# Cross-attention kernel: prompts turned by VectorE, second context chunk turned before the first gram, first x loaded before the keys' weights

## The chip, the core and the metric

The kernel runs on one core of a Trainium2 chip. A core has five engines that run side by side and wait for one another through semaphores: TensorE (PE; its weight loads are shown apart as PEld), VectorE (DVE), ScalarE (ACT), GpSimd (POOL) and SyncE (SP), which here only issues DMAs. The metric is the time of one execution in microseconds (us), lower is better. Everything is float32.

## The reference

Eight batches; each has 112 queries of 320 channels (20 heads of 16) and a context of 375 tokens of 512 channels. The last four tokens of a context are "prompts", the 371 before them are text.

```python
q   = heads(x @ W_q);  k_t = heads(text @ W_k);  v_t = heads(text @ W_v)
probs_t  = softmax(q k_t^T * Dh**-0.5)
text_out = probs_t @ v_t
k_ip = heads(ip @ W_k_ip);  v_ip = heads(ip @ W_v_ip)
qsem = l2norm(probs_t @ text);  ip_n = l2norm(ip)
fused    = q k_ip^T * Dh**-0.5 + 0.5 * (qsem @ ip_n^T)
probs_ip = softmax(fused) * spatial_mask
out = (text_out + probs_ip @ v_ip) @ W_out + b_out + x
```

## The kernel before

**What is computed how.** The norm of `probs_t @ text` is not computed from that product. For each batch the kernel makes a gram matrix of the context tokens (`ctxT` times itself, tile `ug`), in which the four prompt tokens are replaced by their normalised and halved versions. Multiplying the exponentials of the scores with this matrix (the `ps_qd` matmuls, L776) then gives at once what the norms, the prompts' similarities, the softmax sum and the values need.

**Tiles and stages.** Contractions run over partitions, so the context, x and the prompts have to be turned (transposed) first: `ctxT` (512 channels as 128 partitions x 4, by 375 tokens), `xT`, and for the prompts `ipT` (raw, for their keys and values) and `ipnT` (normalised, for the gram). The 32 prompts of all eight batches (`ip_sb`, 32 x 512) are turned once, at the start. The context of batch 0 comes in three chunks of 128 tokens, the last one short (`ct`), each turned by four TensorE transposes into a PSUM bank `ps_c` (L435) and copied out, chunks 0 and 2 by ScalarE (L445), chunk 1 by VectorE (L443). The contexts of the later batches are turned by VectorE in 32 x 32 blocks.

The first gram has one bank for each row of chunks (L474): chunk column 0 needs chunk 0, column 1 chunks 0 and 1, column 2 all three and the prompts' columns, which GpSimd copies from `ipnT` (L468).

**What sets the order.** The order on TensorE, SyncE and VectorE is written out by hand: the prologue is a list of `next(...)` on generators, each of which yields after a piece of work, and an engine runs its instructions strictly in the order in which they were recorded. In the part that the change touches, TensorE does: `awake(4, 168)` (four matmuls on a constant, 168 columns wide, whose result nobody reads; they stand there ahead of the first data), the transposes of chunk 0, those of the raw prompts, the first block of the gram, the transposes of chunks 1 and 2, those of the normalised prompts, the other five blocks of the gram, then the first third of batch 0's queries (L371, from `xT` and `wq_sb`), keys (L568, `wk_sb`), more queries, scores (L705), values (L602, `wv_sb`). A float32 matmul is two entries in the trace, so four matmuls are listed as x8; a transpose is one entry.

All loads of the start but one stand in one SyncE queue: the context of batch 0, `wq_sb`, `wk_sb`, four loads of x into `xr_sb`, `wv_in`, the context of batch 1 (L160, L165). Only `ip_sb` goes through ScalarE's queue.

The kernel's bound in the steady part is TensorE: five groups of heads in each of eight batches, each with scores, `ps_qd` matmuls and, spread in between, the next batch's gram, keys and values. The change touches nothing there.

Of the kernel before, what the change touches and what calls it, by code (L numbers as in the profile page):

```python
# [20 lines left out]
def kernel(  # L21
# [14 lines left out]
    nc = tc.nc  # L36
    P = 128
# [7 lines left out]
    NE = E // P  # L45
# [5 lines left out]
    RG = 32  # L51
# [5 lines left out]
    N = B * NIP  # L57
# [5 lines left out]
    QN = P // RG  # L63
# [21 lines left out]
    def bank(name, spare=False):  # L85

        if spare:
            return ps_sc.tile([P, 512], F32, tag="sc", name=name)
        return ps_mm.tile([P, 512], F32, tag="mm", name=name)
# [22 lines left out]
    ip_sb = const.tile([N, E], F32, tag="ip_sb", name="ip_sb")  # L112
# [5 lines left out]
    def load_pairs(eng, t, w):  # L118

        w = w.rearrange("(p c) f -> p c f", c=5)  # L120
        eng.dma_start(t[0::2, :, :C], w[:, :3, :])
        eng.dma_start(t[1::2, :2, :C], w[:, 3:, :])

    def load_x_blocks(b, j):

        for a in range(QN):
            nc.sync.dma_start(
                xr_sb[a * RG : a * RG + S // QN, j, :, :XB],
                x[b, :, a * XB : (a + 1) * XB].rearrange("(q i) f -> i q f", q=QN),
            )  # L130
# [5 lines left out]
    def load_embed(eng, t, w):  # L136
        eng.dma_start(t[:, :, :C], w.rearrange("(p e) f -> p e f", e=NE))
# [9 lines left out]
    def chunk(t, e):  # L147
        return t.rearrange("t (p e) -> t e p", e=NE)[:, e, :]
# [38 lines left out]
    ident = const.tile([P, P], F32, tag="ident", name="ident")  # L187
# [2 lines left out]
    nc.gpsimd.memset(xr_sb, 0.0)  # L190

    load_pairs(nc.sync, wq_sb, w_q)
    load_embed(nc.sync, wk_sb, w_k)
    load_x_blocks(0, 1)
    load_embed(nc.sync, wv_in, w_v)
    load_ctx_blocks(1)

# [45 lines left out]
    ipT = const.tile([P, NE, N], F32, tag="ipT", name="ipT")  # L243
    ipnT = const.tile([P, NE, N], F32, tag="ipnT", name="ipnT")
# [19 lines left out]

    def normalised_prompts():

        def turned_prompts(src, n):
            ps = bank(f"ps_ipT{n}", spare=True)
            for e in range(NE):
                nc.tensor.transpose(  # L270
                    ps[:, e * N : (e + 1) * N], chunk(src, e), ident[:N, :N]
                )
            return ps[:, : NE * N].rearrange("p (e n) -> p e n", n=N)

        raw = turned_prompts(ip_sb, "r")
        yield

        sq = work.tile([N, E], F32, tag="ipn", name="ipsq", bufs=1)
        ss = small.tile([N, 1], F32, tag="ipss", name="ipss", bufs=1)
        nc.vector.tensor_tensor_reduce(  # L280
            out=sq, in0=ip_sb, in1=ip_sb, scale=1.0, scalar=0.0, op0=ALU.mult, op1=ALU.add,
            accum_out=ss,
        )
        nc.vector.tensor_scalar_max(ss, ss, EPS * EPS)
        rn = small.tile([N, 1], F32, tag="iprn", name="iprn", bufs=1)
        nc.scalar.activation(rn, ss, AF.Sqrt)
        nc.vector.reciprocal(rn, rn)

        ipn = work.tile([N, E], F32, tag="ipn", name="ipn", bufs=1)
        nc.vector.tensor_scalar(ipn, ip_sb, rn, 0.5, op0=ALU.mult, op1=ALU.mult)  # L290
        nc.vector.tensor_copy(ipT, raw)
        yield

        nc.vector.tensor_copy(ipnT, turned_prompts(ipn, "n"))
        yield

    def prompt_projections():
# [119 lines left out]
    def transposed_context(b):  # L417
        begin(b)
        s = st[b]
        ct, ctxT = s["ct"], s["ctxT"]  # L420
        if b > 0:

            for c in range(NT):
                some = slice(c * QN, (c + 1) * QN)
                nc.vector.transpose(  # L425
                    ctxT[:, :, c * P : (c + 1) * P].rearrange("p e (j i) -> p j e i", i=RG),
                    ct[:, some, :].rearrange("p j (k e) -> p j e k", e=NE),
                )
                yield
            return  # L430
        for c in range(NT):
            rows = min(P, TT - c * P)
            ps = bank(f"ps_c_{b}_{c}")
            for e in range(NE):
                nc.tensor.transpose(  # L435
                    ps[:, e * P : e * P + rows],
                    chunk(ct[:, c, :], e)[:rows],
                    ident[:rows, :rows],
                )
            o = ctxT[:, :, c * P : c * P + rows]  # L440
            i = ps.rearrange("p (e t) -> p e t", t=P)[:, :, :rows]
            if c == 1:
                nc.vector.tensor_copy(o, i)  # L443
            else:
                nc.scalar.copy(o, i)  # L445
            yield

    def awake(n, w):

        ps = bank(f"ps_w_{n}", spare=True)  # L450
        one = nc.const_aps.tensor(1.0, [P, w], F32)
        for _ in range(n):
            nc.tensor.matmul(ps[:, :w], one[:, :P], one, start=True, stop=True)
# [7 lines left out]
    def first_gram():  # L461

        ctxT = st[0]["ctxT"]
        banks = []
        for c in range(NT):
            banks.append(ps_qd.tile([P, 512], F32, tag="qd", name=f"ps_g_0_{c}"))
            if c == NT - 1:
                nc.gpsimd.tensor_copy(ctxT[:, :, TT:T], ipnT[:, :, :NIP])  # L468
                for xt in x_ring:
                    nc.gpsimd.memset(xt, 0.0)  # L470
            c0, c1 = c * P, min(c * P + P, T)
            for r in range(c + 1):
                for e in range(NE):
                    nc.tensor.matmul(  # L474
                        banks[r][:, c0 - r * P : c1 - r * P],
                        ctxT[:, e, r * P : (r + 1) * P],
                        ctxT[:, e, c0:c1],
                        start=(e == 0),
                        stop=(e == NE - 1),
                    )  # L480
                if c == NT - 1:
                    doubled(banks[r][:, : T - r * P], r, half[:, 0])
                yield
# [681 lines left out]

    across = [[(a, (a + k) % GROUP) for a in range(GROUP)] for k in range(1, GROUP)]
    prompts = normalised_prompts()
    context = transposed_context(0)
    products = first_gram()
    awake(4, 168)  # L1170
    next(context)
    next(prompts)
    next(prompts)
    next(products)
    next(context)
    next(context)
    next(prompts)
    run(("q", 0), lambda: project_queries(pairs[0]))
# [170 lines left out]
    for g in range(NG):  # L1349
# [6 lines left out]
        for j, _ in enumerate(multiplied(b, g)):  # L1356
# [17 lines left out]
            if g == 1 and j in (2, 3):  # L1374
                for a in ((3, 2), (1, 0))[j - 2]:
                    ps = ps_qd.tile([P, 512], F32, tag="qd", name=f"ps_s_{b}_{NG - 1}_{a}")
# [10 lines left out]
        n = (3, 3, 2, 1)[g]  # L1387
# [91 lines left out]
```

## Time and profile before

| | us |
|---|---|
| median of 3 runs | 414.4 (413.74 to 415.95) |
| the profiled execution's own time | 416.99 |
| its span, first to last instruction | 415.3 |
| first context chunk's transposes start on TensorE | 3.75 |
| first block of the gram starts | 5.53 |
| other blocks of the gram start | 9.77 |
| first queries start | 16.29 |
| VectorE turns x (`xT`) | 12.38 |

Times inside the execution are counted from the span's start. A row of the time line reads: start, time from the first to the end of the last, engine, line, operation, output and input, shape, count, and in brackets how long the engine stood idle before it and what ended that. Matmuls overlap in the pipeline, so one that is listed with 0.42 us may follow the one before it after 0.21 us; the distance of the starts is the pace.

### The profile page before, as it was taken

To read this page: it belongs to the slowest core of one execution; us is meant where nothing else is said; L and a number is where in the kernel's file an instruction comes from. 1 tells how busy PE (TensorE), PEld (TensorE's weight loads), DVE (VectorE), ACT (ScalarE), POOL (GpSimd) and SP (SyncE) were. 2 spreads that over 40 slices of the span, in tenths; PEclk is the share of its full clock that TensorE was granted. 3 is DMA by queue.
4 is the path that set the end of the run, shared out by engine and by line. 5 is a ranking of instruction groups with operands and counts; after the bars stand their busy time and mean duration, and the time that the engine had idled before them with its cause. 6 is when DMAs were issued, how large, how long until landed. Compare 5 with 4: busy or idle time off the path is not lost.

```text
span 415.3 us, 14115 instructions
## 1 busy us (share of the span) xinstructions
PE 409.0 (98%) x5484; PEld 320.7 (77%) x5484; DVE 339.1 (82%) x729; ACT 219.5 (53%) x733; POOL 130.0 (31%) x318
## 2 busy tenths in 40 slices
PE   8999999999999999999999999999999999999995
PEld 7866777788777877788677877788777987787883
DVE  4286788888899979898799988888798977889775
ACT  2364334746365453655448363653637563688773
POOL 4744203112071212612044120702117120545540
PEclk9999999999999999999999999999999999999999
DMA  7647655556654555455555555545544356544300
GB/s 215 149 123 166 203 145 149 138 145 167 173 152 135 153 141 137 115 137 163 138 131 134 138 152 140 149 107 165 140 127 113 95 166 160 131 121 135 104 2 29
DMA packets 46435, 56.95 MB, mean 137 GB/s; under 512 B 9405, under 2 KB 40961, under 8 KB 46368
## 3 DMA queue, kind: packets, MB, share of 16 engines
q1 hardware_dynamic: 46328, 55.99, 50.8%
q8 instruction: 43, 0.70, 0.8%
q14 instruction: 24, 0.20, 0.2%
q10 hardware_dynamic: 40, 0.07, 0.1%
HBM read 15.88 MB, written 1.39 MB: 42 GB/s over the span
## 4 chain that ended last, share of the span: by engine, by line
PE 93%; DVE 3%; DMA 1%; ACT 1%; issue 1%; DVEq 0%
PE ps_qd L776 39%; PE ps_v L602 15%; PE ps_s L705 11%; PE ps_k L568 10%; PE ps_g L518 7%; PE ps_q L371 4%; PE ps_o L993 3%; PE ps_g L474 2%; DVE junk L822 1%; DMA xg<-p 1%; DMA ct<-in_ctx_dram 1%; PE ps_c L435 1%; PE ps_k L584 1%; PE ps_k L559 0%; PE ps_a L981 0%
## 5 line engine op out<-in xcount | busy, mean ns | idle before, releaser
L776 PE MATMUL ps_qd<-u,xgT 32*112 32x168 f32 (+11 forms) x3840 | 216.1, 350 | 0.0
L776 PEld LDWEIGHTS ps_qd<-u,xgT 32*112 32x112 f32 x3840 | 183.8, 172 | 25.9 <-issue 0.5
L741 ACT ACTIVATE p<-ps_s,nmx 112x371 f32<-112x371 f32 x156 | 84.5, 579 | 82.9 <-DVE nmx L727 79.7
L757 DVE STREAM_TRANSPOSE xgT<-xg 128x512 f32<-128x512 f32 (+2 forms) x79 | 126.0, 1602 | 2.4 <-issue 1.8
L727 DVE TENSOR_REDUCE nmx<-ps_s 112x1 f32<-112x371 f32 x160 | 78.8, 537 | 24.7 <-PE ps_s L705 23.5
L822 DVE CUSTOM_DVE_ANT_0 junk<-ps_qd,p 112x371 f32<-112x371 f32 x146 | 79.3, 543 | 19.4 <-ACT pvs L789 3.6
L674 POOL COPY u<-vr 128x64 f32<-128x64 f32 x120 | 26.5, 239 | 140.6 <-PE ps_qd L776 104.1
L705 PE MATMUL ps_s<-kT,qm 32*112 32x375 f32 (+1 forms) x320 | 65.3, 495 | 0.0
L602 PE MATMUL ps_v<-wv_sb,ctxT 128*128 128x384 f32 (+1 forms) x192 | 63.1, 477 | 0.0
L602 PEld LDWEIGHTS ps_v<-wv_sb,ctxT 128*128 128x128 f32 x192 | 35.7, 190 | 21.9 <-DVE qm L381 0.5
L568 PE MATMUL ps_k<-ctxT,wk_sb 128*128 128x371 f32 x136 | 46.6, 487 | 0.0
L705 PEld LDWEIGHTS ps_s<-kT,qm 32*112 32x112 f32 x320 | 25.4, 171 | 12.8 <-issue 10.3
L568 PEld LDWEIGHTS ps_k<-ctxT,wk_sb 128*128 128x128 f32 x136 | 24.5, 189 | 13.5 <-ACT vext L609 0.2
L622 ACT COPY vr<-vext 32x240 f32<-32x240 f32 x88 | 34.2, 389 | 1.3
L609 ACT COPY vext<-ps_v 128x384 f32<-128x384 f32 (+1 forms) x24 | 11.2, 468 | 41.2 <-PE ps_v L602 41.2
L518 PE MATMUL ps_g<-ctxT 128*32 128x375 f32 (+11 forms) x672 | 30.4, 333 | 0.0
L518 PEld LDWEIGHTS ps_g<-ctxT 128*32 128x32 f32 x672 | 27.7, 110 | 2.0
L425 DVE STREAM_TRANSPOSE ctxT<-ct 128x512 f32<-128x512 f32 x21 | 23.1, 1112 | 3.4 <-DMA ct<-in_ctx_dram 3.4
L968 POOL TENSOR_TENSOR wv<-vip,w 112x1280 f32<-112x1280 f32 x6 | 14.8, 2468 | 26.6 <-DVE w L905 26.6
L743 ACT COPY ipl<-ps_s 112x4 f32<-112x4 f32 x140 | 23.1, 165 | 0.0
L490 ACT ACTIVATE ug<-ps_g 128x375 f32<-128x375 f32 (+2 forms) x24 | 8.3, 375 | 26.7 <-PE ps_g L518 10.4
L491 POOL TENSOR_TENSOR ug<-ug,half 128x128 f32<-128x128 f32 (+1 forms) x24 | 10.5, 449 | 29.7 <-ACT ug L490 29.7
(173 smaller groups left out, 348.6 us busy)
## 6 DMA issues: line engine op xcount, KB each, us to landing
xg<-p SPq DMA_DIRECT2D x156, 162.3 KB
u<-ug SPq DMA_DIRECT2D x122, 99.0 KB
ct<-in_ctx_dram SPq DMA_DIRECT2D x28, 176.0 KB
vip<-vipd SPq DMA_DIRECT2D x6, 560.0 KB
xr_sb<-in_x_dram SPq DMA_DIRECT2D x32, 35.0 KB
out_dram<-ob SPq DMA_DIRECT2D x8, 140.0 KB
x_sb<-in_x_dram SPq DMA_DIRECT2D x6, 140.0 KB
xg<-wv_sb SPq DMA_DIRECT2D x4, 162.3 KB
```

The source lines that it names most:

```text
L425: nc.vector.transpose(ctxT[:, :, c * P : (c + 1) * P].rearrange("p e (j i) -> p j e i", i=RG), ct[:, some, :].rearrange("p j (k e) -> p j ...
L518: nc.tensor.matmul(ps[c][q * RG : (q + 1) * RG, j * RG - c * P : T - c * P], ctxT[:, e, j * RG : (j + 1) * RG], ctxT[:, e, j * RG : T], st ...
L568: nc.tensor.matmul(ps[:, :TT], wk_sb[:, e, i * P : (i + 1) * P], s["ctxT"][:, e, :TT], start=(e == 0), stop=(e == NE - 1),)
L602: nc.tensor.matmul(ps[:, :w], ctxT[:, e, c * P : (c + 1) * P], wv_sb[:, e, :w], start=(e == 0), stop=(e == NE - 1),)
L622: copy(s["vr"][a * RG : (a + 1) * RG, q::QN].rearrange("p c g d -> p c (g d)"), s["vext"][q * RG : (q + 1) * RG, :, a * w : (a + 1) * w],)
L674: nc.gpsimd.tensor_copy(v, dealt(b, c, s["vr"][:, c * QN : (c + 1) * QN, g, :]))
L705: nc.tensor.matmul(ps[:S, :w], qm[a * RG : (a + 1) * RG, i, r, j * S : (j + 1) * S], s["kT"][a * RG : (a + 1) * RG, i, :w], start=True, st ...
L727: nc.vector.tensor_reduce(nmx, s["sc", g, a][:S, :TT], AX.X, ALU.max, negate=True)
L741: nc.scalar.activation(s["p", g][:, a, :], ps[:S, :TT], AF.Exp, bias=nmx)
L757: nc.vector.transpose(xT[:, j0:j1].rearrange("p j (k q) -> p q j k", q=QN), xg[:, :, j0 * RG : j1 * RG].rearrange("p q (j k) -> p q j k", ...
L776: nc.tensor.matmul(banks[a][:S, j * RG : UW], xT[a * RG : (a + 1) * RG, j, :S], region(b, c)[a * RG : (a + 1) * RG, q, j * RG - c * P :], ...
L822: nc.vector.tensor_tensor_reduce(out=junk, in0=ps[:S, :TT], in1=s["p", g][:, a, :], scale=1.0, scalar=0.0, op0=ALU.mult, op1=ALU.add, accu ...
```

## The change

Four edits, all ahead of the first scores:

- The prompts are turned by VectorE instead of TensorE. `turned_prompts` was four TensorE transposes into a PSUM bank and one VectorE copy out of it. It is now four VectorE block transposes of 32 x 128 each, which write straight into `ipT` or `ipnT`. As VectorE turns 32 x 32 blocks, 128 neighbouring channels of the prompts land in 32 partitions, one row group for each quarter of the channels. The placing of the channels is as before: channel 4 p + e in partition p, column e.
- Normalised prompts come first, raw ones after them, and the reciprocal and the scaling of the normalised prompts are recorded after the copy of context chunk 1.
- Context chunk 1 is turned ahead of the gram's first block.
- The four loads of x go ahead of `wk_sb` in SyncE's queue, and the four matmuls of `awake` are 200 columns wide instead of 168.

```diff
@@ -190,8 +190,8 @@
     load_pairs(nc.sync, wq_sb, w_q)
+    load_x_blocks(0, 1)
     load_embed(nc.sync, wk_sb, w_k)
-    load_x_blocks(0, 1)
     load_embed(nc.sync, wv_in, w_v)
@@ -264,16 +264,12 @@
-        def turned_prompts(src, n):
-            ps = bank(f"ps_ipT{n}", spare=True)
-            for e in range(NE):
-                nc.tensor.transpose(
-                    ps[:, e * N : (e + 1) * N], chunk(src, e), ident[:N, :N]
+        def turned_prompts(out, src):
+            for a in range(QN):
+                nc.vector.transpose(
+                    out[a * RG : (a + 1) * RG],
+                    src[:, a * P : (a + 1) * P].rearrange("n (p e) -> n e p", e=NE),
                 )
-            return ps[:, : NE * N].rearrange("p (e n) -> p e n", n=N)
-
-        raw = turned_prompts(ip_sb, "r")
-        yield
@@ -284,14 +280,15 @@
         nc.scalar.activation(rn, ss, AF.Sqrt)
+        yield
+
         nc.vector.reciprocal(rn, rn)
-
         ipn = work.tile([N, E], F32, tag="ipn", name="ipn", bufs=1)
         nc.vector.tensor_scalar(ipn, ip_sb, rn, 0.5, op0=ALU.mult, op1=ALU.mult)
-        nc.vector.tensor_copy(ipT, raw)
-        yield
-
-        nc.vector.tensor_copy(ipnT, turned_prompts(ipn, "n"))
+        turned_prompts(ipnT, ipn)
+        yield
+
+        turned_prompts(ipT, ip_sb)
         yield
@@ -1167,12 +1164,12 @@
-    awake(4, 168)
+    awake(4, 200)
     next(context)
     next(prompts)
+    next(context)
+    next(products)
     next(prompts)
-    next(products)
-    next(context)
     next(context)
     next(prompts)
```

TensorE at the program's start, before (`ps_w` is `awake`, `ps_c` the context's transposes, `ps_ipTr` and `ps_ipTn` those of the raw and the normalised prompts, `ps_g` the gram):

```order
L453 MATMUL ps_w_163<-const-float32-1.0 128x168 x4
L435 MATMUL ps_c_0_176<-ident,ct_93 128x128 x4
L270 MATMUL ps_ipTr<-ident,ip_sb 128x32 x4
L474 MATMUL ps_g_0_197<-ctxT_168 128x128 x4
L435 MATMUL ps_c_1_202<-ident,ct_93 128x128 x4
L435 MATMUL ps_c_2_208<-ident,ct_93 128x115 x4
L270 MATMUL ps_ipTn<-ident,ipn 128x32 x4
L474 MATMUL ps_g_0_197<-ctxT_168 128x128 x4
L474 MATMUL ps_g_1_226<-ctxT_168 128x128 x4
```

The same place on TensorE after the change:

```order
L450 MATMUL ps_w_163<-const-float32-1.0 128x200 x4
L432 MATMUL ps_c_0_176<-ident,ct_93 128x128 x4
L432 MATMUL ps_c_1_188<-ident,ct_93 128x128 x4
L471 MATMUL ps_g_0_194<-ctxT_168 128x128 x4
L432 MATMUL ps_c_2_206<-ident,ct_93 128x115 x4
L471 MATMUL ps_g_0_194<-ctxT_168 128x128 x4
L471 MATMUL ps_g_1_222<-ctxT_168 128x128 x4
```

Both groups of prompt transposes are gone from TensorE, and chunk 1 stands where the raw prompts' transposes stood.

VectorE from the prompts' sum of squares to the turning of x, before:

```order
L280 ISA ipsq,ipss<-ip_sb 32x512
L280 ISA ipss 32x1
L284 TENSOR_SCALAR ipss<-ipss 32x1
L287 RECIPROCAL iprn<-iprn 32x1
L290 TENSOR_SCALAR ipn<-ip_sb,iprn 32x512
L291 COPY ipT<-ps_ipTr 128x128
L443 COPY ctxT_168<-ps_c_1_202 128x4x128
L294 COPY ipnT<-ps_ipTn 128x128
L359 STREAM_TRANSPOSE xT_220<-xr_sb 128x128 x3
```

The same place on VectorE after the change:

```order
L276 ISA ipsq,ipss<-ip_sb 32x512
L276 ISA ipss 32x1
L280 TENSOR_SCALAR ipss<-ipss 32x1
L440 COPY ctxT_168<-ps_c_1_188 128x4x128
L285 RECIPROCAL iprn<-iprn 32x1
L287 TENSOR_SCALAR ipn<-ip_sb,iprn 32x512
L269 STREAM_TRANSPOSE ipnT<-ipn 32x128 x4
L269 STREAM_TRANSPOSE ipT<-ip_sb 32x128 x4
L356 STREAM_TRANSPOSE xT_216<-xr_sb 128x128 x3
```

Two copies out of PSUM became eight block transposes, and the copy of chunk 1 now stands ahead of the reciprocal.

## The prediction

> **What bounds the kernel now.** I read the page first: busy times and the chain that ended last.
>
> ```profile
> span 415.3 us, 14115 instructions
> PE 409.0 (98%) x5484; PEld 320.7 (77%) x5484; DVE 339.1 (82%) x729; ACT 219.5 (53%) x733; POOL 130.0 (31%) x318
> PE 93%; DVE 3%; DMA 1%; ACT 1%; issue 1%; DVEq 0%
> ```
>
> TensorE carries 93% of the chain. The waits of TensorE's matmuls and its busy time in two later stretches tell whether anything holds it after the start:
>
> ```profile
> PE ps_q L371 <- ACT ipl L743: 0.7, 1, 0.7
> PE ps_wT L1080 <- DVE w_last L1075: 0.7, 1, 0.7
> PE ps_c L435 <- DMA ct<-in_ctx_dram: 0.3, 1, 0.3
> ...
> 17.12:100.00 82.88, 82.16 (x1070) 1.00 0.60 152
> 100.00:400.00 300.00, 300.00 (x4230) 1.00 0.51 135
> ```
>
> After 17.12 us TensorE lacks 0.72 us up to 400. So a microsecond won before 17 us should arrive at the end whole, unless a producer that does not move with TensorE comes late. Next, the time line of TensorE to that point:
>
> ```profile
> 0.85 2.58 PE L453 MATMUL ps_w<-const-float32-1.0 128*128 128x168 f32 x8 [0.85 <-PEq L1461]
> 3.75 1.10 PE L435 MATMUL ps_c<-ident,ct 128*128 128x128 f32 x4 [0.32 <-DMA ct<-in_ctx_dram]
> 4.79 0.68 PE L270 MATMUL ps_ipTr<-ident,ip_sb 32*128 32x32 f32 x4
> 5.53 2.08 PE L474 MATMUL ps_g<-ctxT 128*128 128x128 f32 x8
> 7.40 1.83 PE L435 MATMUL ps_c<-ident,ct 128*128 128x128 f32 x8
> 9.16 0.68 PE L270 MATMUL ps_ipTn<-ident,ipn 32*128 32x32 f32 x4
> 9.77 6.68 PE L474 MATMUL ps_g<-ctxT 128*128 128x128 f32 x40
> 16.29 0.83 PE L371 MATMUL ps_q<-xT,wq_sb 128*128 128x112 f32 x6
> 16.95 2.67 PE L568 MATMUL ps_k<-ctxT,wk_sb 128*128 128x371 f32 x8
> ```
>
> It looks full, but its pace is not even. Two stretches of the 40 gram matmuls (16 of 128 columns, then 24 of 119), and the durations of all 48:
>
> ```profile
> 10.14 3.19 PE L474 MATMUL ps_g<-ctxT 128*128 128x128 f32 x14
> ...
> 14.17 2.29 PE L474 MATMUL ps_g<-ctxT 128*128 128x119 f32 x19
> ...
> L474 PE MATMUL ps_g<-ctxT x48: 274/421/582, 5.5 to 16.2; 128*128 128x128 f32 x24, 128*128 128x119 f32 x24
> ```
>
> Early pace: (3.19 - 0.42) / 13 = 0.213 us at 128 columns, so 0.199 at 119. Late pace: (2.29 - 0.275) / 18 = 0.112 at 119, so 0.120 at 128. TensorE runs at about half speed first. The first of the 40 takes 0.16 longer (its weights cannot be loaded ahead), so the 16 wide ones end at 9.77 + 0.16 + 16 x 0.213 = 13.35; the other 24 take 2.94, which fits 2.9 slow and 21.1 fast ones: the speed changes at 13.9 us. The granted clock in the windows reads 1.00 all along and does not show this; the pace does.
>
> **What released the speed.** By these rows full-width work ran unbroken from 5.53 to 9.16 (3.6 us) without release; then came four transposes of 32 columns (ps_ipTn), then full-width work from 9.77 to 13.9 (4.1 us), and release. So a run of more than 3.6 and at most 4.1 us seems to be asked for, which the two small groups cut short.
>
> **The change part by part.** TensorE first. *Awake* of 200 columns: before, eight entries fill 0.85 to about 3.22 ((2.58 - 0.49) / 7 = 0.28 to 0.30 each); 200/168 of that ends near 3.65. Its cover is the wait for the first chunk, up to 3.75: cost 0. If that chunk landed at once it would cost 0.43.
>
> *Chunk 1 into the gap.* The gram's first block waits for ScalarE's copy of chunk 0, and chunk 1 now needs its own load:
>
> ```profile
> 4.89 0.59 ACT L445 COPY ctxT<-ps_c 128x512 f32<-128x512 f32 x1 [1.49 <-PE ps_c L435]
> ...
> L435 PEldq EVENT_SEMAPHORE  x2: 51/51/51, 3.6 to 5.8; - x2
> ...
> 4.00:5.00 1.00, 1.00 (x6) 0.67 (x5) 0.82 (x3) 0.11 (x1) 0.77 (x10) 1.00 0.80 266
> ```
>
> The weight loader's waits for chunks 0 and 2 ended at 3.6 and 5.8; chunk 1 (256 KB) is between them. Estimate: 256 KB at 266 GB/s is 1.0 us, so about 4.7, and the matmul 0.1 to 0.2 later: 4.9. Bounds: 4.6 (landed in time) and 5.9 (with chunk 2). Four chunk transposes take (9.16 - 7.40) / 2 = 0.88, so chunk 1 ends at 5.78, past ScalarE's copy (5.48). The first gram block takes 7.40 - 5.53 = 1.87: ends 7.65. Chunk 2: 8.53. The 40 gram matmuls then start at 8.53 instead of 9.77, and without the 0.16, since no small transposes stand ahead. The removed raw transposes gain nothing: they lay in the gap.
>
> *Release.* No small group is left after 5.78. With a run of 4.1 us the speed comes at 9.9 (3.6 would be 9.4; counted from chunk 1 it is 8.5 to 9.0). By 9.9, 1.37 / 0.213 = 6.4 wide ones are done; 9.6 x 0.120 + 24 x 0.112 = 3.84, so queries start at 13.74 instead of 16.29: **2.55 us gained**. With chunk 1 at 5.9 everything and the release move by 1.0: 1.55; at 4.6: 2.85.
>
> VectorE now does eight transposes. Its rows before:
>
> ```profile
> 5.37 0.20 ACT L286 ACTIVATE iprn<-ipss 32x1 f32<-32x1 f32 x1
> ...
> 5.61 0.15 DVE L287 RECIPROCAL iprn<-iprn 32x1 f32<-32x1 f32 x1 [0.75 <-ACT iprn L286]
> 5.79 0.47 DVE L290 TENSOR_SCALAR ipn<-ip_sb,iprn 32x512 f32<-32x512 f32 x1
> 8.50 0.69 DVE L443 COPY ctxT<-ps_c 128x512 f32<-128x512 f32 x1 [2.03 <-PE ps_c L435]
> 12.38 0.75 DVE L359 STREAM_TRANSPOSE xT<-xr_sb 128x128 f32<-128x128 f32 x3 [2.21 <-DMA xr_sb<-in_x_dram]
> ...
> L425 DVE STREAM_TRANSPOSE ctxT<-ct x21: 1075/1105/1145, 22.9 to 310.5; 128x512 f32<-128x512 f32 x21
> ...
> 10.23 0.20 POOL L468 COPY ctxT<-ipnT 128x16 f32<-128x16 f32 x1 [5.03 <-DVE ipnT L294]
> ```
>
> A 32 x 128 transpose is not in the trace. Nearest: 0.25 each (L359: also 128 elements a partition, also read with a stride), and as the other end 1.10 (L425, four times the elements). I take 0.25. Behind chunk 1's copy (5.9 to 6.6) stand reciprocal and scaling (7.2), ipnT (8.2), ipT (9.2). GpSimd's copy of the prompt columns is done near 8.5; the gram asks for it at its 17th matmul, near 11. Cost 0. Behind ipT waits the turning of x: 9.2 to 10.0, if x is there, needed at 13.74.
>
> SyncE's queue. The rows that tell when the moved loads landed:
>
> ```profile
> 4.28 0.61 SPq L137 DMA_DIRECT2D wk_sb<-in_L_xattn_W_k_dram  x1
> 5.00 1.84 SPq L127 DMA_DIRECT2D xr_sb<-in_x_dram  x4
> ...
> SPq L160 <- DMA wk_sb<-in_L_xattn_W_k_dram: 2.7, 1, 2.7
> SPq L165 <- DMA wv_in<-in_L_xattn_W_v_dram: 1.8, 1, 1.8
> ...
> 11.04 0.82 SPq L160 DMA_DIRECT2D ct<-in_ctx_dram  x2
> ...
> 14.69 0.23 SPq L165 DMA_DIRECT2D ct<-in_ctx_dram  x1
> ...
> 17.65 0.78 DVE L256 COPY wv_sb<-wv_in 128x512 f32<-128x512 f32 x2
> 22.93 3.11 DVE L425 STREAM_TRANSPOSE ctxT<-ct 128x512 f32<-128x512 f32 x3
> ```
>
> Keys' weights landed by 11.04, x by 12.38. Swapped, the weights land by 12.4 at worst: the same bytes lie ahead of that point. Keys start 0.66 after the queries, at 14.4: 2.0 us of cover. x comes earlier, and at its old 12.38 would still be turned by 13.13. So the swap gains nothing by itself and costs nothing; without it x would have 0.6 us of cover. The values' weights landed by 14.69; VectorE orders them 0.49 after its first query copies begin, at 15.1: 0.4 us of cover, and if it is gone, VectorE's 1.55 us idle time ahead of its next query copies takes it. Batch 1's context is asked for at 22.93, then at 20.4; its last load was issued at 14.69.
>
> Sum for the profiled execution: 416.99 - 2.55 = 414.4. Its own time is 2.6 us over the median of the runs; the difference carries over, so 414.4 - 2.6 = **411.8 us**. No change is what lies within 0.5%, 2.07 us, about what a measurement of this kernel can tell.
>
> **The rivals.**
>
> *A fixed beat.* If the release comes only at the end of a beat of its own that was busy throughout, a beat b of 3 to 4.1 us ended at 13.9; the one before it, at 9.8 to 10.9, would now be busy too. At 10.5 the queries start at 14.0 and the gain is 2.3; in other executions the beat falls elsewhere, before and after alike, and a median of few runs may show 1.5 to 3.7. [...]
>
> *The release stays at 13.9*, because transposes or the 0.3 us pause ahead of chunk 1 matter in a way that I do not see. Then 16 wide ones end at 11.94, 9.8 narrow ones at 13.9, the rest at 15.49: gain 0.8, 413.6. For it: a release was seen once only.
>
> *Release near 4.6 to 5.0*, because awake and chunk 0 now join (pause 0.1 instead of 0.5) into a run of 3.6 to 4.1 us. Then chunk 1 ends at 5.4, the gram's first block at 6.5, chunk 2 at 7.0, the gram at 11.6: gain 4.7, 409.7. Against it: the pause ahead of chunk 1.
>
> *VectorE makes it slower.* x is turned behind the eight transposes: 7.2 + 8 d + 0.75. It delays the queries past 13.74 for d over 0.72, and past the old 16.29 for d over 1.04; at 1.10 they start at 16.75 and the time is 414.9; 0.5% slower needs d of 1.3. Against it: L359's 0.25.
>
> *Lost later.* The loads that do not move (values' weights, batch 1's context) or the order of transfers take most of the gain back: 413.5 to 414.4. Against it: the 22.93 row had no wait for its load.
>
> **How the numbers follow.** Release by run or by beat: 62%, of this four fifths and more beyond 2.07 us (51 points; 11 within). Early release 7%. Release unmoved 15%, within 0.5%. Lost later 8% (6 within, 2 slower). VectorE 4% (half slower). Something slow that I have not named 4%. Faster 0.58, same 0.34, slower 0.08. The range takes in the early release (409.7) and, above, the lost gain: 409.6 to 414.4; the likeliest case alone spans 410.7 to 412.9 (gains of 3.7 to 1.5).
>
> **What the profile would show.** Gram matmuls 0.112 to 0.120 apart from about 9.9 on; chunk 1's transposes from 4.9; queries near 13.7 and the whole rest of TensorE 2.5 us earlier; eight transposes of 0.25 us. It is wrong if the change of pace is found near 13.9 still, if the queries wait for xT, or if TensorE gains idle time after 17 us.

## The result

| | before | after |
|---|---|---|
| median, us | 414.5 (413.74 to 416.45, 8 runs) | 411.86 (411.36 to 413.74, 8 runs) |
| ratio | | 0.9929, 95% interval 0.9905 to 0.9953 |
| profiled execution: time, span | 416.99, 415.3 | 412.23, 410.5 |
| queries start on TensorE | 16.29 | 12.51 |
| span from there on | 399.0 | 398.0 |

The change is 0.7% faster, and 411.8 was forecast. The two profiled executions lie 4.8 us apart, though, and the medians 2.6; that the forecast gave the second number has a weaker reason than its sum suggests, as the experiments show.

TensorE of the changed kernel to the keys, in the time line:

```profile
0.85 3.00 PE L450 MATMUL ps_w<-const-float32-1.0 128*128 128x200 f32 x8 [0.85 <-PEq L1458]
3.65 1.03 PE L432 MATMUL ps_c<-ident,ct 128*128 128x128 f32 x4
5.69 0.75 PE L432 MATMUL ps_c<-ident,ct 128*128 128x128 f32 x4 [1.01 <-DMA ct<-in_ctx_dram]
6.28 1.06 PE L471 MATMUL ps_g<-ctxT 128*128 128x128 f32 x8
7.17 0.63 PE L432 MATMUL ps_c<-ident,ct 115*128 115x115 f32 x4
7.63 5.04 PE L471 MATMUL ps_g<-ctxT 128*128 128x128 f32 x40
12.51 0.83 PE L368 MATMUL ps_q<-xT,wq_sb 128*128 128x112 f32 x6
13.17 2.67 PE L565 MATMUL ps_k<-ctxT,wk_sb 128*128 128x371 f32 x8
```

Four transposes of chunk 0 take 1.03 us, those of chunk 1 0.75; the gram's first block takes 1.06 instead of 2.08. So TensorE is at full pace from chunk 1 on. The trace's record of the granted clock, of which the windows print 1.00, begins at 4.5 us here and at 13.9 in the kernel before, just where the pace changes: what comes ahead of it is not recorded, and was slow. The moment at which this record begins is called the release below.

VectorE and GpSimd at that place:

```profile
6.48 0.69 DVE L440 COPY ctxT<-ps_c 128x512 f32<-128x512 f32 x1 [1.59 <-PE ps_c L432]
7.09 0.14 DVE L285 RECIPROCAL iprn<-iprn 32x1 f32<-32x1 f32 x1
7.26 0.47 DVE L287 TENSOR_SCALAR ipn<-ip_sb,iprn 32x512 f32<-32x512 f32 x1
7.77 1.65 DVE L269 STREAM_TRANSPOSE ipnT<-ipn 32x128 f32<-32x128 f32 x4
9.45 1.64 DVE L269 STREAM_TRANSPOSE ipT<-ip_sb 32x128 f32<-32x128 f32 x4
11.12 0.75 DVE L356 STREAM_TRANSPOSE xT<-xr_sb 128x128 f32<-128x128 f32 x3
...
9.48 0.20 POOL L465 COPY ctxT<-ipnT 128x16 f32<-128x16 f32 x1 [4.29 <-DVE ipnT L269]
```

A 32 x 128 transpose takes 0.41 us (1.65 / 4). The gram's 17th matmul follows the 16th after 0.41 us instead of 0.11, just behind GpSimd's copy of the prompt columns (9.48 + 0.20): a pause of 0.3 us for them. x is turned right behind the prompts, with no wait for its load.

After the start nothing was lost. TensorE's waits, and its busy time in the stretches that the prediction showed:

```profile
PE ps_c L432 <- DMA ct<-in_ctx_dram: 1.0, 1, 1.0
PE ps_w L450 <- PEq L1458: 0.9, 1, 0.9
PE ps_wT L1077 <- DVE w_last L1072: 0.7, 1, 0.7
...
17.12:100.00 82.88, 82.88 (x1092) 1.00 0.61 156
100.00:400.00 300.00, 300.00 (x4267) 1.00 0.50 133
```

### The profile page after: what moved, and what is told of

Read it like the earlier page. It is cut to its first block, busy times and chain, and to the rows that moved or that the text cites. A ratio compares the mean times of both kernels' runs of the same rounds, so it can differ in the third digit from the quotient of the medians.

```text
span 410.5 us, 14104 instructions
## 1 busy us (share of the span) xinstructions
PE 404.2 (98%) x5476; PEld 316.4 (77%) x5476; DVE 341.2 (83%) x735; ACT 219.7 (54%) x733; POOL 129.6 (32%) x318
## 4 chain that ended last, share of the span: by engine, by line
PE 95%; DVE 2%; DMA 1%; ACT 1%; issue 0%; SPq 0%; POOL 0%; DVEq 0%
PE ps_qd L773 42%; PE ps_v L599 15%; PE ps_k L565 11%; PE ps_s L702 11%; PE ps_g L515 7%; PE ps_q L368 4%; PE ps_o L990 3%; DMA ct<-in_ctx_dram 1%; PE ps_g L471 1%; PE ps_k L581 1%; PE ps_k L556 0%; PE ps_a L978 0%; DVE ipnT L269 0%; PE ps_ipkv L306 0%; ACT L1409 0%; DVE junk L819 0%
## 5 line engine op out<-in xcount | busy, mean ns | idle before, releaser
L702 PEld LDWEIGHTS ps_s<-kT,qm 32*112 32x112 f32 x320 | 25.4, 171 | 12.8 <-issue 10.3
L565 PEld LDWEIGHTS ps_k<-ctxT,wk_sb 128*128 128x128 f32 x136 | 24.5, 189 | 13.5 <-ACT vext L606 0.2
L606 ACT COPY vext<-ps_v 128x384 f32<-128x384 f32 (+1 forms) x24 | 11.2, 468 | 41.2 <-PE ps_v L599 41.2
```

Of the source, the lines that this page charges most:

```text
L565: nc.tensor.matmul(ps[:, :TT], wk_sb[:, e, i * P : (i + 1) * P], s["ctxT"][:, e, :TT], start=(e == 0), stop=(e == NE - 1),)
L702: nc.tensor.matmul(ps[:S, :w], qm[a * RG : (a + 1) * RG, i, r, j * S : (j + 1) * S], s["kT"][a * RG : (a + 1) * RG, i, :w], start=True, st ...
```

## The experiments

Twelve kernels in three batches, each batch on its own chip beside the kernel before. Its medians there were 414.13, 413.83 and 414.02, so a comparison within a batch, or by the ratio to it, is the safe one.

### One part at a time, and the kernel before again

**The kernel before, unchanged.**

> The kernel before, unchanged, for a second profile of it. Beat theory (the speed is released at the end of a beat that runs free of the kernel, so the release moves from execution to execution): the pace changes at another time than 13.9 us, and the profiled time follows it, about 0.5 us for each us of release; a release near 10 gives about 415. Run theory (a full-width run of 3.6 to 4.1 us releases): the pace changes at 13.4 to 13.9 again and the profiled time is 416.5 to 417 again. Median 414.5 by both.

Measured: 414.1. Its profiled execution took 414.1, and the pace changed elsewhere:

```profile
7.22 1.83 PE L435 MATMUL ps_c<-ident,ct 128*128 128x128 f32 x8
8.98 0.66 PE L270 MATMUL ps_ipTn<-ident,ipn 32*128 32x32 f32 x4
9.57 4.72 PE L474 MATMUL ps_g<-ctxT 128*128 128x128 f32 x40
14.13 0.83 PE L371 MATMUL ps_q<-xT,wq_sb 128*128 128x112 f32 x6
```

The 40 gram matmuls take 4.72 instead of 6.68 us: all at full pace. The clock record begins at 9.2. The run theory (a full-width run of 3.6 to 4.1 us releases), under which 13.4 to 13.9 would have come again, falls; the release moves from execution to execution of the same kernel. 4.7 us of release are worth 2.2 us in the queries' start.

The 90 runs of the kernel before in the three batches show the same thing without a profile: 29 lie at 412.05 to 413.31 (median 412.5), 42 at 413.44 to 415.10 (414.1), 19 at 415.71 to 416.55 (416.0). The groups' medians are 1.6 and 1.9 us apart; half of the 3.41 us by which the clock records differ in length (below) would be 1.7. The first two groups nearly touch (413.31 and 413.44), so their border is drawn by eye. The execution on which the prediction was built belonged to the slowest group.

**Awake, narrow in the changed kernel.**

```diff
-    awake(4, 200)
+    awake(4, 168)
```

> The changed kernel with the awake matmuls 168 columns wide again, so that the pause of 0.4 to 0.5 us ahead of the first chunk is back. If the release at 4.5 us in the changed kernel's profile came from awake and chunk 0 joined without a pause, it is lost here: release at 9 to 13 and a median of 412.5 to 413.5 (0.7 to 1.5 us over the changed kernel's 411.9). If the gain is the transposes that were removed and moved, the width of awake does not matter: 411.9, within 0.4.

Measured: 411.61, ratio to before 0.9930 (0.9904 to 0.9957), as the changed kernel. The pause is back (0.17 us with a wait for chunk 0 in this profile), the clock record begins at 5.8. The width does not matter here.

**Awake, wide in the kernel before.**

```diff
-    awake(4, 168)
+    awake(4, 200)
```

> The kernel before with awake 200 columns wide, nothing else. If closing the pause brings the early release, this alone gains: in executions where the release comes near 4.5 about 3 us, in others nothing, so a median of 412 to 414. If the gain is the work removed and moved: 414.5, within 0.4.

Measured: 414.05, ratio 0.9990 (0.9963 to 1.0017): a hair outside both expected ranges, with the three groups as before (5, 3 and 4 of 12 runs). Its profile is one of an early release (4.2), and shows what then binds:

```profile
7.90 4.72 PE L474 MATMUL ps_g<-ctxT 128*128 128x128 f32 x40
12.97 0.89 PE L371 MATMUL ps_q<-xT,wq_sb 128*128 128x112 f32 x6 [0.35 <-PE ps_g L474]
...
12.54 0.74 DVE L359 STREAM_TRANSPOSE xT<-xr_sb 128x128 f32<-128x128 f32 x3 [4.25 <-DMA ct<-in_ctx_dram]
```

The queries stood still for 0.35 us, though the gram was done at 12.62. VectorE had waited 4.25 us for a DMA and turned x only at 12.54; x is loaded behind the keys' weights here.

**Chunk 1 ahead of the gram's first block, alone.** In the list of the kernel before:

```diff
-    next(products)
     next(context)
+    next(products)
     next(context)
```

> The kernel before with chunk 1 turned ahead of the gram's first block, nothing else: prompts stay on TensorE. Work theory: chunk 1 fills the gap, gain of 0.1 to 0.4 us (0.88 of work against a wait for chunk 1's load up to 5.7 and the raw prompts' transposes still in the gap): 414.1 to 414.4. Release theory: the small transposes still stand ahead of the main gram, so the release stays late: the same 414.1 to 414.5.

Measured: 413.8, ratio 0.9982 (0.9954 to 1.0010), three groups as before (5, 4 and 3 of 12 runs).

**Prompts by VectorE, alone.** The normalised prompts come first here too, and the four TensorE transposes are gone:

```diff
...
+        def turned_prompts(out, src):
+            for a in range(QN):
+                nc.vector.transpose(
...
-        nc.vector.tensor_copy(ipT, raw)
+        turned_prompts(ipnT, ipn)
...
-        nc.vector.tensor_copy(ipnT, turned_prompts(ipn, "n"))
+        turned_prompts(ipT, ip_sb)
```

> The kernel before with the prompts turned by VectorE, nothing else: chunk 1 after the gram's first block, x behind the keys' weights, awake 168 wide. The runs of before fall into three groups, about 412.5, 414.1 and 416.2, a half beat of speed (1.7 us) apart. If the small transposes spoil beats (release theory), the third group and much of the second go: a median of 412 to 412.6, and hardly a run over 414.5. If only their 0.6 us of work counts (work theory), the three groups stay with their shares, each 0.3 to 0.6 lower: a median of 413.5 to 413.8.

Measured: 413.87, ratio 1.0013 (0.9996 to 1.0030). Neither theory's median. The slowest group nearly goes (1 run of 12 over 415.3), the middle one stays. The profile shows the reason:

```profile
5.48 2.08 PE L472 MATMUL ps_g<-ctxT 128*128 128x128 f32 x8 [0.68 <-ACT ctxT L443]
7.35 1.83 PE L433 MATMUL ps_c<-ident,ct 128*128 128x128 f32 x8
9.20 4.98 PE L472 MATMUL ps_g<-ctxT 128*128 128x128 f32 x40
```

With the raw prompts gone and chunk 1 not yet moved, TensorE waits 0.68 us for chunk 0's copy. Removing the small transposes alone leaves that gap.

### One part taken back out of the changed kernel

**x behind the keys' weights.**

```diff
-    load_x_blocks(0, 1)
     load_embed(nc.sync, wk_sb, w_k)
+    load_x_blocks(0, 1)
```

> The changed kernel with x behind the keys' weights again. x is then ready at 12.4 to 13.1 as before. My prediction had this worth nothing with a release at 9.9; with a release near 4 to 6, where the queries could start at 11.6 to 12.5, they now wait: 0.5 to 1.3 us, a median of 412.3 to 413. If the loads' order is worth nothing: 411.7, within 0.4.

Measured: 412.25, ratio 0.9976 (0.9953 to 0.9998). It lies 0.3 to 0.4 us over the changed kernel's medians (411.86 and 411.91, on other chips), just under what was expected if the queries wait for x, and three of 12 runs are over 413.2. The profiled execution is one of these three (413.29), and it does not show x as the cause:

```profile
5.32 1.13 PE L432 MATMUL ps_c<-ident,ct 128*128 128x128 f32 x4 [0.61 <-DMA ct<-in_ctx_dram]
...
13.39 0.83 PE L368 MATMUL ps_q<-xT,wq_sb 128*128 128x112 f32 x6
...
11.23 0.76 DVE L356 STREAM_TRANSPOSE xT<-xr_sb 128x128 f32<-128x128 f32 x3
```

x is turned without a wait at 11.23 and the queries start 1.4 us after that is done; the release came only at 9.1. The median may mean that the loads' order is worth some tenths, but that is not shown, and the intervals of the two ratios overlap.

**Chunk 1 behind the gram's first block.**

```diff
-    next(context)
     next(products)
+    next(context)
```

> The changed kernel with chunk 1 turned after the gram's first block again. By my sum the move is worth about 0.8 us at slow pace (0.88 of work into a gap of 0.7, less the wait for its load), and about 0.1 at full pace, where the load of chunk 1 is what is waited for: a median of 411.9 to 412.7. If a pause ahead of the gram's first block (4.7 to 5.4, nothing to do) also spoils beats, later releases come back and the median is over 412.7.

Measured: 414.07, ratio 1.0005 (0.9987 to 1.0024): the whole gain is gone, as was expected if a pause there spoils beats. 7 of 12 runs are at 414.1 to 414.3, 5 at 412.5 to 412.8. TensorE waits 0.68 us ahead of the gram's first block again, and in this order VectorE's reciprocal stands behind a copy of chunk 1 that cannot start before 8.35, so the normalised prompts come late as well:

```profile
5.38 2.08 PE L471 MATMUL ps_g<-ctxT 128*128 128x128 f32 x8 [0.68 <-ACT ctxT L442]
...
8.35 0.69 DVE L440 COPY ctxT<-ps_c 128x512 f32<-128x512 f32 x1 [4.08 <-PE ps_c L432]
9.65 1.63 DVE L269 STREAM_TRANSPOSE ipnT<-ipn 32x128 f32<-32x128 f32 x4
12.98 0.76 DVE L356 STREAM_TRANSPOSE xT<-xr_sb 128x128 f32<-128x128 f32 x3
```

The run does not tell these two apart.

**The wait for chunk 1 filled.**

```diff
     next(prompts)
+    awake(1, 128)
     next(context)
```

> The changed kernel with one more constant matmul of 128 columns between chunk 0 and chunk 1 (0.43 us at slow pace, 0.24 at full pace), in the wait for chunk 1's load. If pauses spoil beats, none is left from 0.85 on and the runs near 413.5 (2 of 17 with the changed kernel and its narrow version) go: median 411.3 to 411.9, highest under 412.6. If the pause does not matter: the same 411.7 and one run in eight near 413.5.

Measured: 411.82, ratio 0.9959 (0.9941 to 0.9978), highest 412.85. No run near 413.5 in 12; the changed kernel itself had one in 15. The median is where it was expected, the highest run is above the 412.6 that was expected, and 12 runs cannot show that those near 413.5 are gone.

**Small transposes back on TensorE.**

```diff
+    def small_group(n):
+        ps = bank(f"ps_small_{n}", spare=True)
+        for e in range(NE):
+            nc.tensor.transpose(ps[:, e * N : (e + 1) * N], ident[:N, :], ident[:N, :N])
+
     next(context)
     next(prompts)
+    small_group(0)
     next(context)
     next(products)
     next(prompts)
     next(context)
+    small_group(1)
     next(prompts)
```

> The changed kernel with two groups of four 32-column transposes of a constant back on TensorE, one between chunk 0 and chunk 1 (in the wait for chunk 1's load), one between chunk 2 and the rest of the gram; nobody reads them. Work theory: only the second costs, 0.35 to 0.6 us: a median of 412.1 to 412.4 and the same narrow spread. Release theory: the second group also spoils the beats that hold it; with a release near 4 to 9 before it in most executions it costs the same 0.35 to 0.6 there, and in the rest the runs go to 413.5 and above: a median of 412.2 to 413, and at least one run in six over 413.2.

Measured: 412.08 (0.2 us over the changed kernel on the same chip; 11 of 12 runs at 411.85 to 412.86, one at 413.69), ratio 0.9963. In the profile the second group holds 0.36 us (7.33 to 7.69):

```profile
4.66 0.63 PE L1171 MATMUL ps_small<-ident 32*128 32x32 f32 x4
5.22 0.81 PE L432 MATMUL ps_c<-ident,ct 128*128 128x128 f32 x4
...
7.33 0.43 PE L1171 MATMUL ps_small<-ident 32*128 32x32 f32 x4
7.69 4.72 PE L471 MATMUL ps_g<-ctxT 128*128 128x128 f32 x40
```

Here the work theory is right: the small transposes by themselves cost about their work or less, 0.2 us in the medians, and with everything else of the change in place they hardly ever delay the release: one run of 12 is over 413.2, where two or more were expected if they do.

**No awake at all, in the kernel before.**

```diff
-    awake(4, 168)
```

> The kernel before without the awake matmuls, whose result nobody reads. Release theory: the beats that end near 4 are idle without them, so the fastest of the three groups (about 412.4, a third of the runs) is empty: all runs at 413.8 and above, a median of 414.2 to 415.5. If awake does nothing: three groups and 414.

Measured: 415.76 (413.56 to 416.52), ratio 1.0034 (1.0010 to 1.0059). The fastest group is empty (lowest run 413.56), 7 of 11 runs are in the slowest, and the median is even above the 415.5 that was expected. Matmuls whose result nobody reads are worth 1.7 us of median, so the release theory holds where the work theory predicts nothing.

### The changed kernel again, and one with two more edits

> The changed kernel again, for a second profile and its spread beside the others. Release theory: another release time than 4.5 us, and queries that start between 11.2 and 13.7 accordingly; median 411.8, one run in eight or ten near 413.5.

Measured: 411.91 (411.41 to 412.06, 7 runs), ratio 0.9955 (0.9935 to 0.9975). The clock record begins at 6.8 us, the queries at 12.13. No run of the seven is near 413.5. Here chunk 1's load did not keep TensorE waiting:

```profile
3.83 2.21 PE L432 MATMUL ps_c<-ident,ct 128*128 128x128 f32 x8
5.84 1.50 PE L471 MATMUL ps_g<-ctxT 128*128 128x128 f32 x8
```

The ratio is nearer to 1 than the first one (0.9929). The eight runs of the kernel before in the first comparison held none of its fastest group (the lowest is 413.74), of which there are 29 among the later 90; so 0.7% is on the high side. The median of the 90 is 414.0, and 411.9 against that is 0.5%, though on different chips.

**The fill, and chunk 1 copied by ScalarE.**

```diff
-            if c == 1:
-                nc.vector.tensor_copy(o, i)
-            else:
-                nc.scalar.copy(o, i)
+            nc.scalar.copy(o, i)
...
     next(prompts)
+    awake(1, 128)
     next(context)
```

> The changed kernel with the constant matmul between chunk 0 and chunk 1 (as in the filled kernel) and chunk 1 copied by ScalarE instead of VectorE, so that VectorE's reciprocal, scaling and turning of the normalised prompts do not stand behind it. In the changed kernel's profile TensorE paused 0.3 us for the prompt columns and VectorE's turning of x ended 0.6 us ahead of the queries. If that chain binds in executions with an early release: 0.2 to 0.5 us gained, a median of 411.2 to 411.6. If not: 411.8.

Measured: 411.45 (411.07 to 412.06, 6 runs), ratio 0.9953 (0.9936 to 0.9970). Against the changed kernel on the same chip the median is 0.46 us lower, as expected if the chain binds; but the two ratios to before do not differ, so a gain over the changed kernel is not shown. The prompts' chain is off TensorE's path:

```profile
6.19 1.66 DVE L269 STREAM_TRANSPOSE ipnT<-ipn 32x128 f32<-32x128 f32 x4
...
7.91 0.20 POOL L462 COPY ctxT<-ipnT 128x16 f32<-128x16 f32 x1 [2.72 <-DVE ipnT L269]
...
6.94 4.63 PE L468 MATMUL ps_g<-ctxT 128*128 128x128 f32 x40
11.41 0.83 PE L368 MATMUL ps_q<-xT,wq_sb 128*128 128x112 f32 x6
```

The prompt columns are there at 8.1, the gram takes 4.63 us instead of 5.04, and the queries start at 11.41, the earliest of all profiles.

## Why the prediction was right, and where it was not

All fourteen profiles side by side. The second column is where the trace's clock record begins. The next two give how much of the 3.41 us (a beat, below) up to that moment, and of the 3.41 us before them, TensorE's matmuls filled, each counted by its columns at the slow pace (0.213 us for 128); time ahead of the program's first matmul counts as idle.

| kernel | release, us | beat before it | the beat earlier | queries start | span from there |
|---|---|---|---|---|---|
| before, first profile | 13.9 | 1.00 | 0.79 | 16.29 | 399.0 |
| before, again | 9.2 | 0.93 | 0.64 | 14.13 | 398.2 |
| wide awake alone | 4.2 | 0.92 | - | 12.97 | 398.6 |
| chunk 1 first alone | 4.1 | 0.78 | - | 12.44 | 398.6 |
| prompts alone | 9.8 | 0.89 | 0.54 | 14.02 | 398.2 |
| no awake | 13.5 | 0.98 | 0.82 | 16.08 | 398.0 |
| chunk 1 back | 10.3 | 0.89 | 0.69 | 14.36 | 398.0 |
| x back | 9.1 | 0.99 | 0.74 | 13.39 | 398.2 |
| changed | 4.5 | 0.96 | 0.07 | 12.51 | 398.0 |
| changed, again | 6.8 | 0.86 | 0.69 | 12.13 | 398.2 |
| narrow awake | 5.8 | 0.82 | 0.41 | 11.63 | 398.0 |
| filled | 5.5 | 1.00 | 0.31 | 11.87 | 398.2 |
| small ones back | 5.6 | 0.83 | 0.34 | 12.25 | 398.0 |
| fill and ScalarE's copy | 4.7 | 0.97 | 0.10 | 11.41 | 398.2 |

**A microsecond won ahead of the queries arrives whole: right.** From the queries on the span is 398.0 to 399.0 in every kernel. The 399.0 is the execution on which the prediction was built; 0.7 of it is the wait for `ipl` shown there, which recurs in one other profile alone (0.4 us, chunk 1 first).

**What released the speed: wrong in its rule.** I read one execution and took a full-width run of 3.6 to 4.1 us to be needed. The rival of a fixed beat is what fits the runs. The trace's record of full clock is 399.36 us long in the first profile of the kernel before, 406.19 in the first of the changed kernel, and 399.36, 402.77 or 406.19 in the twelve others: steps of 3.41 us, and 117, 118 or 119 times 3.4133 (399.36 / 117). By these lengths it begins and ends on a beat of 3.41 us.

The beat does not start with the kernel. Divided by 3.4133, the releases leave remainders of 0.25 and 2.34 us in the two profiles of the kernel before, and of 1.10 and 3.34 in the two of the changed kernel. In the execution that I read, counted back from 13.9, beats ended at 7.08 and 10.49, so the full-width run from 5.53 to 9.16 filled neither of them. The rival's beat of 3 to 4.1 us and its 10.5 were estimates that no row of the profile before fixes; these lengths give 3.41 us and 10.49.

How full a beat must be is not shown. By the table each release ends a beat that was filled to 0.78 or more, and the beat just before that one was filled to 0.82 at most. The two ranges overlap (0.78 released, 0.79 and 0.82 did not), so a bound near 0.8 is an estimate, and the columns are a rough measure of whatever is counted.

**Where the beats were spoiled: half right.** The two small groups were named. In all profiles with the kernel before's order or with a part alone, the release comes at 4.1 to 4.2 or at 9.2 and later, never between; the beats that end between hold the wait for chunk 0's copy and, where they are still on TensorE, the raw prompts' transposes. I had costed exactly that place at nothing ("they lay in the gap"), which holds for their time, not for the release. With small transposes back in an otherwise changed kernel the release came at 5.6 all the same; with x back, where TensorE's order is that of the changed kernel, it came at 9.1, and the beat that ended at 5.7 (filled to 0.74) held the 0.61 us wait for chunk 1's load. So no single culprit is seen: that pauses and small transposes of one beat add up fits all of this, and each part alone (chunk 1 first, prompts by VectorE, wide awake) left enough of them for ratios of 0.998 to 1.001, whereas the whole gave 0.993 and, on another chip, 0.996. Of the parts taken back, awake's width cost nothing, x some tenths at most, chunk 1 everything. Whether prompts by VectorE and chunk 1 first suffice as a pair was not run.

**The difference carries over (414.4 less 2.6): right number, wrong step.** The profiled execution had a late release, 13.9, and was 2.5 us over the median mostly for that reason; the sum moved the release from 13.9 to 9.9 and so gained 2.55. Profiled executions near the median of the kernel before have it at 9.2 to 10.3 (414.1, and 413.96 and 414.07 with prompts alone and chunk 1 back), and those of the changed kernel at 4.5 and 6.8. That step is of about the same length, one beat's worth, at another place. That the forecast met the median is in good part luck. Where the release is early in both, the change gains less: the fastest group of the kernel before has a median of 412.5, against 411.9.

**Chunk 1's load: at its bound.** 4.9 was taken, 5.9 was the bound; the changed kernel's first profile has 5.69, in the other profiles with chunk 1 first it starts at 4.5 to 5.3. In the first profile this wait of 1.01 us ate part of the earlier release (a gain of 3.8 in the queries' start where the rival with a release at 4.6 to 5.0 had 4.7).

**VectorE at no cost: wrong in size.** The term "I take 0.25" measured 0.41 us for each transpose; the nearest row was neither of the two I chose between, but inside the bounds. The prompt columns came at 9.7 instead of 8.5, and the gram asked for them at 9.4 instead of 11, since it ran at full pace: 0.3 us. Turned x had 0.6 us to spare (11.87 to 12.51), not 3.7.

**The swap of the loads worth nothing: right only for a late release.** With the old order VectorE begins to turn x at 11.2 to 12.5 in the profiles. That is in time for queries at 13.4 or later, but cost 0.35 us in the wide-awake profile, with queries at 12.97. What the swap is worth in the median of the changed kernel is not shown.

**Awake at no cost: right** (ratio 0.9990 alone, and a median of 411.61 against 411.86 when taken back).

## What to carry to other kernels

Where the first microseconds of a TensorE-bound kernel run at half pace, look for what delays the release, and price a change there by what one beat more at half pace costs (1.7 us here, half of 3.41; the groups of runs lie 1.6 and 1.9 us apart) times the share of executions in which it decides, not by the time of the instructions it removes. A profile is one execution: before building a sum on it, hold its time against the spread of the runs, and ask to which group it belongs. Here, once the start was faster, TensorE waited 1.01 us for chunk 1's load and 0.3 us for the prompt columns, and turned x had 0.6 us to spare instead of 3.7, so the order of loads and side chains should be settled together with the start.

## What was not expected of the hardware

- The times of one kernel fall into groups 1.6 to 1.9 us apart (29, 42 and 19 of 90 runs). The two profiles of that kernel, at 416.99 and 414.1, have releases at 13.9 and 9.2; that the release makes all three groups is inferred, as no profile was taken of those 90.
- The clock column reads 1.00 also ahead of the release; the pace of equal matmuls tells it: 0.213 us for 128 columns ahead of it, (1.06 - 0.275) / 7 = 0.112 in the first gram block after. That is the pace of the 119 columns too, so the 0.120 that I scaled up for the wide ones was a little high.
- A VectorE transpose of 32 x 128 takes 0.41 us, more than one of 128 x 128 (0.21 to 0.25 us apart in the same trace, with the same elements in a partition).
